# Layer 1's attention weights: transposed by VectorE in 32x32 squares and moved by transfers, mixed two blocks late

## The chip, the core and the metric

The kernel runs on one core of a Trainium2 chip. TensorE does matrix products into PSUM; VectorE (DVE), ScalarE (ACT) and GpSimd (POOL) do the rest; SyncE (SP), ACT and POOL also issue DMA transfers, each from its own in-order instruction queue. The metric is the device time of one execution in microseconds (us). Before the change its median was 2407.27 us over three runs (2404.34 to 2408.37).

## The reference

The input `x` is 8 batches of 256 channels on a 32x32 image, so 1024 tokens of 256 values in each batch, all in float32. Two layers follow each other.

Layer 0 is a linear attention block with 8 heads of 64, a softmax over the query index, an output projection and a residual. Layer 1 first normalizes each token and attends over the batch's own tokens, then adds a mixture of 8 experts with the best two for each token:

```python
def _L1_attn_ref(x, W):
    xa = jnp.einsum('bnd,ed->bne', x, W)
    scores = jnp.einsum('bne,bme->bnm', xa, x)
    attn = jax.nn.softmax(scores, axis=-1)
    y = jnp.einsum('bnm,bmd->bnd', attn, x)
    return y
...
t = _to_tokens(x)
t = t + _L1_attn_ref(_ln_t(t), L1_attn_W)
t = t + _L1_ffn_ref(_ln_t(t), L1_ffn_router_w, ...)
```

The change concerns `attn` in these lines: a 1024x1024 matrix in each batch. The product with `x` sums over the keys `m`, and TensorE sums over partitions, while the softmax sums over the free dimension. So the weights are made with the queries on partitions and are needed with the keys on partitions: they must be transposed.

## The kernel before, in words

A batch goes through layer 0 (`layer0`), layer 1's attention (`attend`), and the normalization and routing for the experts (`normed`, `dispatch`). Batches 0 to 6 send their tokens to the experts' rows in HBM; `experts` then runs once for all seven, and the last batch is done densely (`dense`) while the experts' results of the others are gathered, added and stored (`Results`).

`attend` splits the batch's 1024 queries into `NT = 8` blocks of 128. For a block `i`, `scores(i)` makes 128x1024 scores on TensorE in a PSUM tile of two banks (L670; the pool `ps_big` has three such tiles), VectorE takes the negated maximum of each row (`nmax`, L678), and ScalarE writes the exponentials to SBUF with their row sums (`ex`, L681, in the pool `expp`, which has six buffers of 128x1024 under the tag `exps`). `mix(i)` then has TensorE transpose the eight 128x128 squares of `ex` into a PSUM tile (`pa`, L689), VectorE copies them to SBUF (`aT`, L691), and TensorE makes eight products with the normalized tokens `n1` (`py`, L695). VectorE divides by the row sums and adds the residual (L699, L701). The loop at the end of `attend` runs `scores(i)` before `mix(i - 1)`, so a block is mixed one block late.

The token order inside a block is not the image's: a block of `NB = 4` has the tokens of one half of the batch (`NH2 = 2` halves of 512) that are congruent modulo 4. It makes 32x32 squares of the input and output images into transposes of VectorE: `SQ = 32`, `NQ = 4` groups of 32 partitions. `load_squares` and `residual` (L427, L434) and `store` (L1186, L1193) already use that.

`fill` calls put other work between: in batches 0 to 6 the next batch's value and query projections (`Begin.at`, lines `pv` L387 and `pqk` L328), in batch 7 the gathering and adding of the experts' results. The framework schedules the traced instructions into each engine's order and writes the semaphores. Every transfer issued from SP or ACT adds to one of eight semaphores, which are used in turn, and waits before it is issued until the transfer before it on the same semaphore has landed. In layer 0 of batches 1 to 7, SP also relays between TensorE's instructions (`relay`, L555).

Of the kernel before, what the change touches and what calls it, by code (L numbers as in the profile page):

```python
# [10 lines left out]
F32 = mybir.dt.float32  # L11
# [8 lines left out]
def kernel(  # L20
# [23 lines left out]
    nc = tc.nc  # L44
    P = 128
    B, C, S = x.shape
    E, D, FF = w1.shape
# [4 lines left out]
    NT = S // P  # L52
    NH2 = S // 512
# [14 lines left out]
    expp = ctx.enter_context(tc.tile_pool(name="expp", bufs=6))  # L68
# [6 lines left out]
    def big(name):  # L75

        return ps_big.tile([P, 1024], F32, tag="big", name=name)

    def acc(name):

        return ps_acc.tile([P, 512], F32, tag="acc", name=name)
# [54 lines left out]
    for e in range(E):  # L136
# [30 lines left out]
        fill=0.0,  # L167
# [41 lines left out]
    NB = NT // NH2  # L209
    SQ = 32  # L210
    NQ = P // SQ
# [40 lines left out]
    def layer_norm(t, dst, eps, name):  # L252
        return Norm(t, dst, eps, name).blocks(0, NT)

    def to_channels(t, dst, name):

        for cc in range(NCC):
            pt = big(f"pt_{name}_{cc}")
            for i in range(NT):
                nc.tensor.transpose(pt[:, ts(i, P)], t[:, i, ts(cc, P)], ident)  # L260
            copied = nc.vector.tensor_copy(dst[:, cc, :], pt)
        return copied
# [380 lines left out]
    def attend(b, t1, fill, tick=nothing):  # L643
        n1 = one.tile([P, NT, D], F32, tag="n", name=f"n1_{b}")
        layer_norm(t1, n1, 1e-5, f"a{b}")
        fill("norm 1")
        nT = one.tile([P, NCC, S], F32, tag="nT", name=f"nT_{b}")
        to_channels(n1, nT, f"n1_{b}")
        fill("normed 1")
        xa = one.tile([P, NCC, S], F32, tag="xa", name=f"xa_{b}")  # L650
        for ec in range(NCC):
            px = big(f"px_{b}_{ec}")
            for dc in range(NCC):
                for n in range(NH2):
                    nc.tensor.matmul(  # L655
                        px[:, ts(n, 512)],
                        WT[:, dc, ts(ec, P)],
                        nT[:, dc, ts(n, 512)],
                        start=(dc == 0),
                        stop=(dc == NCC - 1),  # L660
                    )
            tick(("xa", ec), nc.vector.tensor_copy(xa[:, ec, :], px))

        t2 = t1

        def scores(i):
            psc = big(f"ps1_{b}_{i}")
            for ec in range(NCC):
                for n in range(NH2):
                    nc.tensor.matmul(  # L670
                        psc[:, ts(n, 512)],
                        xa[:, ec, ts(i, P)],
                        nT[:, ec, ts(n, 512)],
                        start=(ec == 0),
                        stop=(ec == NCC - 1),
                    )
            nmax = small.tile([P, 1], F32, tag="nmax", name=f"nmax_{b}_{i}")
            tick(("max", i), nc.vector.tensor_reduce(nmax, psc, AX.X, ALU.max, negate=True))  # L678
            ex = expp.tile([P, 1024], F32, tag="exps", name=f"ex1_{b}_{i}")
            ssum = small.tile([P, 1], F32, tag="ssum", name=f"ssum_{b}_{i}")  # L680
            nc.scalar.activation(ex, psc, AF.Exp, bias=nmax, scale=1.0, accum_out=ssum)  # L681
            return ex, ssum

        def mix(i, ex, ssum):
            if i == NT - 1:
                fill("last weights")
            pt = big(f"pa_{b}_{i}")
            for m in range(NT):
                nc.tensor.transpose(pt[:, ts(m, P)], ex[:, ts(m, P)], ident)  # L689
            aT = two.tile([P, S], F32, tag="tr", name=f"aT_{b}_{i}")  # L690
            nc.vector.tensor_copy(aT, pt)  # L691
            ahead = fill("last products") if i == NT - 1 else None
            py = acc(f"py_{b}_{i}")
            for m in range(NT):
                nc.tensor.matmul(  # L695
                    py[:, :D], aT[:, ts(m, P)], n1[:, m, :], start=(m == 0), stop=(m == NT - 1)
                )
            rs = small.tile([P, 1], F32, tag="rs1", name=f"rs1_{b}_{i}")
            nc.vector.reciprocal(rs, ssum)  # L699
            with tc.issue_after(ahead.ins) if ahead else nullcontext():  # L700
                mixed = nc.vector.scalar_tensor_tensor(  # L701
                    t2[:, i, :], py[:, :D], rs, t1[:, i, :], ALU.mult, ALU.add
                )
            tick(("mixed", i), mixed)

        pending = None
        for i in range(NT):
            now = (i, *scores(i))
            if pending is not None:
                mix(*pending)  # L710
            pending = now
        mix(*pending)
        return t2


# [87 lines left out]
    def normed(b, t2, fill, tick=nothing, norm=None):  # L803

        if norm is None:
            n2 = one.tile([P, NT, D], F32, tag="n", name=f"n2_{b}")
            tick("normed", layer_norm(t2, n2, 1e-5, f"f{b}"))
        else:
            n2 = norm.dst
            tick("normed", norm.blocks(NT - 1, NT))  # L810
        fill("norm 2")
        nT = one.tile([P, NCC, S], F32, tag="nT", name=f"n2T_{b}")
        tick("turned", to_channels(n2, nT, f"n2_{b}"))

        nc.gpsimd.tensor_add(t2, t2, n2)  # L815
        fill("normed 2")
        l = logits(b, nT)
        return n2, nT, l
# [256 lines left out]
    class Results:  # L1075
# [94 lines left out]
        def tick(self, place, behind=None):  # L1170
            added, sent, stored = self.PLACES.get(place, (0, 0, 0))
            if added:
                with tc.issue_after(behind.ins):
                    for _ in range(added):
                        self.add()
            for _ in range(sent):
                self.gather(behind)
            for _ in range(stored):
                if self.whole:
                    b, total, n = self.whole.pop(0)  # L1180
                    store(b, total, n)
# [130 lines left out]
    for b in range(B):  # L1312
        xT = next_x
        if b + 1 < B:
            next_x = load_x(b + 1)
        if b > 0:
            xs = load_squares(b)
        t1 = layer0(b, xT, begun, routing, xs)
        if b + 1 < B:
            begun = Begin(b + 1, next_x)  # L1320
            t2 = attend(b, t1, begun.at)
            n2, _, l = normed(b, t2, begun.at)
            nc.sync.dma_start(groups[0].sums[b], t2)
            routing = dispatch(b, n2, l, groups[0])
            continue
        experts(groups[0])
        others = Results(groups[0])
        others.begin()
        norm = None

        def fill(place):

            nonlocal norm
            others.tick(place)
            if place == "last products":
                norm = Norm(t1, one.tile([P, NT, D], F32, tag="xa", name=f"n2_{b}"), 1e-5, f"f{b}")
                return norm.blocks(0, NT - 1)

        t2 = attend(b, t1, fill, others.tick)
        dense(b, t2, norm, others.tick)  # L1340
        assert others.added == len(others.units) and not others.whole
# [42 lines left out]
```

## Time and profile before

| what | value |
|---|---|
| median of three runs | 2407.27 us |
| the profiled execution | 2406.31 us |
| its span, first to last instruction | 2404.6 us |
| TensorE busy | 2359.7 us, 98% of the span |
| VectorE busy | 1540.9 us, 64% |
| ScalarE busy | 938.0 us, 39% |
| TensorE clock granted | 0.994 of full speed |
| transposes of the weights (`pa`) | 512 instructions, 273 ns each from start to end, overlapping |
| copies of them (`aT`) | 64 of 128x1024, median 1215 ns |
| one block of `attend`, batches 0 to 6 | 7.88 us |

Profile rows give the start in us from the span's beginning, the time, the engine, the line of the kernel, the operation, and the tiles written and read. PE is TensorE's products and PEld its weight loads; SPq and ACTq are instructions of a queue, such as the issue of a transfer. An arrow `<-` at the end says what released the engine from its wait. Each product of float32 appears as two MATMUL records. A time to landing goes from the issue until the data has arrived.

### The profile page before, as it was taken

The numbers are of one execution on the slowest core, as the hardware profiler recorded it, in microseconds if no ns is written. First come the engines' busy times: TensorE is split into PE (matmuls) and PEld (weight loads), VectorE is DVE, ScalarE is ACT, GpSimd is POOL, SyncE is SP. The second block draws the span as 40 slices with busy tenths as digits, with TensorE's granted clock in tenths as the row PEclk, the third lists the DMA queues.
The fourth block names the chain that finished last, engine by engine and source line by source line (L and its number), as shares of the span: only waits on it lengthen the run. The fifth ranks groups of instructions, "written<-read, shape, count | busy, mean of one in ns | idle before, by whom it ended". The sixth has DMA issues, their size and how long they took to land.

```text
span 2404.6 us, 36813 instructions
## 1 busy us (share of the span) xinstructions
PE 2359.7 (98%) x13759; PEld 1316.5 (55%) x13759; DVE 1540.9 (64%) x3660; ACT 938.0 (39%) x1570; POOL 420.0 (17%) x391
## 2 busy tenths in 40 slices
PE   9999999999999999999999999999999999999898
PEld 3356534654466336633664356435653388887565
DVE  5775587457845785578647864687468753334776
ACT  3651366126611662156315641465136622221111
POOL 0000012000200020003000200020002234444563
PEclk9999999999999999999999999999999999999899
DMA  8993201010101010001000100100010256665454
GB/s 294 386 386 101 53 19 36 1 36 12 43 1 35 8 47 1 18 18 54 1 18 18 47 8 6 31 25 12 1 36 19 74 176 220 219 219 161 142 170 119
DMA packets 114778, 196.59 MB, mean 82 GB/s; under 512 B 15752, under 2 KB 58408, under 8 KB 112808
## 3 DMA queue, kind: packets, MB, share of 16 engines
q1 hardware_dynamic: 88504, 126.52, 15.8%
q0 software_dynamic: 25008, 67.20, 9.1%
q8 instruction: 109, 1.79, 0.3%
q10 hardware_dynamic: 1088, 0.52, 0.1%
q14 instruction: 69, 0.57, 0.1%
HBM read 108.88 MB, written 110.90 MB: 91 GB/s over the span
## 4 chain that ended last, share of the span: by engine, by line
PE 91%; DVE 5%; ACT 2%; DMA 1%; issue 1%; POOL 0%; SPq 0%; DVEq 0%; ACTq 0%; POOLq 0%
PE po L545 19%; PE psc L468 18%; PE py L695 9%; PE ps L670 7%; PE pqk L350 7%; PE pr L636 5%; PE ph L1021 4%; PE pv L387 4%; PE pe L1046 4%; PE pdh L1250 2%; PE px L655 2%; PE pdy L1274 2%; PE pa L689 2%; PE pqk L328 2%; PE px L1011 1%
## 5 line engine op out<-in xcount | busy, mean ns | idle before, releaser
L509 ACT ACTIVATE ex<-psc,nmax 128x1024 f32<-128x1024 f32 x512 | 570.5, 1115 | 312.6 <-DVE scrap L492 227.8
L468 PE MATMUL psc<-qk,qk 64*64 64x512 f32 x4096 | 578.4, 594 | 10.3 <-ACT ex L509 10.3
L545 PE MATMUL po<-ex,vs 64*64 64x512 f32 x4096 | 573.5, 592 | 1.3 <-DVE vs L525 0.3
L492 DVE TENSOR_SCALAR_CACHE_REDUCE scrap<-psc,nmax 128x512 f32<-128x512 f32 x512 | 384.4, 751 | 152.0 <-PE psc L468 126.2
L483 DVE TENSOR_REDUCE nmax<-psc 128x1 f32<-128x512 f32 x512 | 350.3, 684 | 9.3 <-PE psc L468 9.3
L468 PEld LDWEIGHTS psc<-qk,qk 64*64 64x64 f32 x4096 | 181.0, 132 | 285.8 <-ACT ex L509 138.0
L545 PEld LDWEIGHTS po<-ex,vs 64*64 64x64 f32 x4096 | 177.9, 132 | 273.5 <-issue 81.7
L695 PE MATMUL py<-n,aT 128*128 128x256 f32 x1024 | 238.0, 386 | 2.9 <-DVE aT L691 2.9
L670 PE MATMUL ps<-nT,xa 128*128 128x512 f32 x512 | 236.0, 592 | 0.0
L695 PEld LDWEIGHTS py<-n,aT 128*128 128x128 f32 x1024 | 191.7, 191 | 66.6 <-DVE aT L691 41.8
L884 POOL DMA_INDIRECT rows<-n,d_at x112 | 108.8, 972 | 662.6 <-DVE nmax L483 662.3
L681 ACT ACTIVATE ex<-ps,nmax 128x1024 f32<-128x1024 f32 x64 | 71.3, 1115 | 348.0 <-DVE nmax L678 333.5
L815 POOL TENSOR_TENSOR t<-t,n 128x2048 f32<-128x2048 f32 x8 | 36.3, 4534 | 924.0 <-DVE n L242 924.0
L350 PE MATMUL pqk<-xT,wqkv 128*128 128x512 f32 x384 | 171.2, 599 | 0.0
L701 DVE SCALAR_TENSOR_TENSOR t<-py,rs,t 128x256 f32<-128x256 f32 x64 | 30.9, 482 | 194.4 <-PE py L695 194.4
L670 PEld LDWEIGHTS ps<-nT,xa 128*128 128x128 f32 x512 | 93.5, 190 | 81.2 <-issue 75.1
L350 PEld LDWEIGHTS pqk<-xT,wqkv 128*128 128x128 f32 x384 | 71.0, 190 | 99.9 <-issue 77.8
L1130 POOL DMA_INDIRECT yk<-y,yat x112 | 110.6, 988 | 72.4 <-issue 26.8
L636 PEld LDWEIGHTS pr<-wo,res 128*128 128x128 f32 x512 | 120.7, 331 | 3.7 <-ACT res L563 3.7
L636 PE MATMUL pr<-wo,res 128*128 128x256 f32 x512 | 121.6, 398 | 0.3 <-ACT res L563 0.3
L387 PE MATMUL pv<-wqkv,xT 128*128 128x512 f32 x256 | 120.3, 599 | 1.4 <-DVE v L395 1.0
L315 ACT ACTIVATE qk<-pqk,b_qks 128x512 f32<-128x512 f32 x124 | 85.6, 691 | 88.9 <-PE pqk L350 79.8
(189 smaller groups left out, 2479.8 us busy)
## 6 DMA issues: line engine op xcount, KB each, us to landing
rows<-wb SPq DMA_DIRECT2D x7, 8192.0 KB, 51.7
y<-yb SPq DMA_DIRECT2D x63, 256.0 KB, 2.4
xs<-in_x_dram SPq DMA_DIRECT2D x64, 128.0 KB, 3.9
out_dram<-oT SPq DMA_DIRECT2D x60, 128.0 KB, 2.9
xT<-in_x_dram SPq DMA_DIRECT2D x7, 1024.0 KB, 5.0
sums<-t SPq DMA_DIRECT2D x7, 1024.0 KB, 3.9
o<-sums SPq DMA_DIRECT2D x7, 1024.0 KB
wpack<-in_L_ffn_w_dram SPq DMA_DIRECT2D x4, 1024.0 KB
```

Source lines behind the costliest of these rows:

```text
L350: mm = nc.tensor.matmul(pq[:, ts(n, 512)], wqkv[:, cc, t, ts(g, P)], xT[:, cc, ts(n, 512)], start=(cc == 0), stop=(cc == NCC - 1),)
L387: nc.tensor.matmul(pv, self.xT[:, cc, ts(i, P)], wqkv[:, cc, 2, :], start=(cc == 0), stop=(cc == NCC - 1),)
L468: mm = nc.tensor.matmul(pss[at, h][ts(c, DK), ts(n, 512)], k[r, j * P + c * DK : j * P + (c + 1) * DK], q[r, ts(n, 512)], start=True, stop ...
L483: firsts[at, h] = nc.vector.tensor_reduce(nmax, pss[at, h][:, ts(0, 512)], AX.X, ALU.max, negate=True)
L492: seconds[h] = nc.vector.tensor_scalar(scrap, pss[at, h][:, ts(1, 512)], -1.0, nmaxes[at, h], ALU.mult, ALU.min, accum_out=nmax,)
L509: nc.scalar.activation(ex, pss.pop((at, h)), AF.Exp, bias=nmaxes.pop((at, h)), scale=1.0, accum_out=sums[at][:, h : h + 1],)
L545: mm = nc.tensor.matmul(po[n][ts(h, DK), :], vss[at][keys, h, :], exps[at, h][keys, ts(n, 512)], start=(j == 0 and turn == 0), stop=(j == ...
L636: nc.tensor.matmul(pr[:, :C], own(res[:, g, :], i), wo[:, g, :], start=(g == 0), stop=(g == NPAIR - 1))
L670: nc.tensor.matmul(psc[:, ts(n, 512)], xa[:, ec, ts(i, P)], nT[:, ec, ts(n, 512)], start=(ec == 0), stop=(ec == NCC - 1),)
L695: nc.tensor.matmul(py[:, :D], aT[:, ts(m, P)], n1[:, m, :], start=(m == 0), stop=(m == NT - 1))
L884: scatter = nc.gpsimd.indirect_dma_start(out=view[:, :], out_offset=bass.IndirectOffsetOnAxis(ap=ats[k][:, i : i + 1], axis=0), in_=n2[:, ...
L1130: ins = nc.gpsimd.indirect_dma_start(out=self.slot(at)[:, k, :], out_offset=None, in_=self.group.y[:, :], in_offset=bass.IndirectOffsetOnAxis(
```

## The change

The first seven blocks of a batch are transposed by `turn` rather than by TensorE. VectorE transposes each 32x32 square of `ex` in two instructions of 128x512, into a tile `sq`. Inside each square that is a full transpose, but the squares are still on the partitions of their old rows. Sixteen transfers of 32 partitions x 2 halves x 128 values move them to their places in a tile `aT`: those of row groups 0 and 2 are issued by SP, those of 1 and 3 by ACT. `mix` reads its eight 128x128 operands from `aT` with a stride. `ex`, `sq` and `aT` all come from the six buffers of the tag `exps`. A block is mixed two blocks late; the eighth block of a batch is transposed by TensorE as before (`turn_last`), after the loop.

```diff
-        def mix(i, ex, ssum):
-            if i == NT - 1:
-                fill("last weights")
+        def turn(i, ex):
+            sq = expp.tile([P, S], F32, tag="exps", name=f"sq_{b}_{i}")
+            to = sq.rearrange("p (n a q m) -> p n m a q", n=NH2, a=NQ, q=SQ)
+            since = ex.rearrange("p (n m a k) -> p n m a k", n=NH2, a=NQ, k=SQ)
+            for n in range(NH2):
+                nc.vector.transpose(to[:, n], since[:, n])
+            aT = expp.tile([P, S], F32, tag="exps", name=f"aT_{b}_{i}")
+            to, since = (t.rearrange("p (n c) -> p n c", n=NH2) for t in (aT, sq))
+            for a in range(NQ):
+                queue = (nc.sync, nc.scalar)[a % 2]
+                for k in range(NQ):
+                    queue.dma_start(to[ts(k, SQ), :, ts(a, P)], since[ts(a, SQ), :, ts(k, P)])
+            by = aT.rearrange("p (n q m) -> p n m q", n=NH2, q=P)
+            return [by[:, m // NB, m % NB] for m in range(NT)]
+
+        def turn_last(i, ex):
             pt = big(f"pa_{b}_{i}")
             for m in range(NT):
                 nc.tensor.transpose(pt[:, ts(m, P)], ex[:, ts(m, P)], ident)
             aT = two.tile([P, S], F32, tag="tr", name=f"aT_{b}_{i}")
             nc.vector.tensor_copy(aT, pt)
+            return [aT[:, ts(m, P)] for m in range(NT)]
+
+        def mix(i, aT, ssum):
             ahead = fill("last products") if i == NT - 1 else None
             py = acc(f"py_{b}_{i}")
             for m in range(NT):
                 nc.tensor.matmul(
-                    py[:, :D], aT[:, ts(m, P)], n1[:, m, :], start=(m == 0), stop=(m == NT - 1)
+                    py[:, :D], aT[m], n1[:, m, :], start=(m == 0), stop=(m == NT - 1)
                 )
...
-        pending = None
+        pending = []
         for i in range(NT):
-            now = (i, *scores(i))
-            if pending is not None:
-                mix(*pending)
-            pending = now
-        mix(*pending)
+            ex, ssum = scores(i)
+            if i < NT - 1:
+                pending.append((i, turn(i, ex), ssum))
+            if i > 1:
+                mix(*pending.pop(0))
+        fill("last weights")
+        pending.append((NT - 1, turn_last(NT - 1, ex), ssum))
+        for some in pending:
+            mix(*some)
```

## The prediction

> **What bounds the kernel now.** I read the page first: the engine totals and the chain that ended last.
>
> ```profile
> PE 2359.7 (98%) x13759; PEld 1316.5 (55%) x13759; DVE 1540.9 (64%) x3660; ACT 938.0 (39%) x1570; POOL 420.0 (17%) x391
> PE 91%; DVE 5%; ACT 2%; DMA 1%; issue 1%; POOL 0%; SPq 0%; DVEq 0%; ACTq 0%; POOLq 0%
> PE po L545 19%; PE psc L468 18%; PE py L695 9%; PE ps L670 7%; PE pqk L350 7%; PE pr L636 5%; PE ph L1021 4%; PE pv L387 4%; PE pe L1046 4%; PE pdh L1250 2%; PE px L655 2%; PE pdy L1274 2%; PE pa L689 2%; PE pqk L328 2%; PE px L1011 1%
> ```
>
> TensorE is the bound, and the work to be removed (`pa` L689) is 2% of its chain. So the first question is what the transposes cost TensorE, the second whether anything slower takes their place. Next I read the timeline of one block of layer 1's attention, in batch 0.
>
> ```profile
> 213.10 1.04 PE L689 MATMUL pa<-ident,ex 128*128 128x128 f32 x8
> 213.30 1.23 DVE L678 TENSOR_REDUCE nmax<-ps 128x1 f32<-128x1024 f32 x1 [0.56 <-PE ps L670]
> 213.97 1.88 PE L670 MATMUL ps<-nT,xa 128*128 128x512 f32 x4
> 214.44 1.22 DVE L691 COPY aT<-pa 128x1024 f32<-128x1024 f32 x1
> 215.71 3.72 PE L695 MATMUL py<-n,aT 128*128 128x256 f32 x16
> 219.27 1.88 PE L670 MATMUL ps<-nT,xa 128*128 128x512 f32 x4
> 220.98 1.04 PE L689 MATMUL pa<-ident,ex 128*128 128x128 f32 x8
> ```
>
> A block takes 7.88 us (213.10 to 220.98), all TensorE: eight transposes 0.87 (213.10 to 213.97), scores 3.4, products 3.4. VectorE is busy 3.6 of it and ScalarE 1.2, so both have room. Then ScalarE alone in the same batch: first two and last exponentials.
>
> ```profile
> 204.02 1.11 ACT L681 ACTIVATE ex<-ps,nmax 128x1024 f32<-128x1024 f32 x1
> 205.04 0.19 ACT L681 ACTIVATION_READ_ACCUMULATOR ex<-ps,nmax 128x1 f32 x1
> 206.18 1.12 ACT L681 ACTIVATE ex<-ps,nmax 128x1024 f32<-128x1024 f32 x1 [0.95 <-DVE rs L699]
> ...
> 254.04 1.11 ACT L681 ACTIVATE ex<-ps,nmax 128x1024 f32<-128x1024 f32 x1 [6.68 <-DVE nmax L678]
> ```
>
> Exponential 7 starts 50.0 us after exponential 0, in every batch; it waits for TensorE, never the reverse. Last, the rows nearest to the new operations: the store's transpose, four small transfers in a row on SP, two times to landing (of L1060, 256 KB, and of `out_dram`, 128 KB), and a wait of SP on an older transfer.
>
> ```profile
> L1186 DVE STREAM_TRANSPOSE oT<-o x14: 1941/2022/2120, 2218.0 to 2381.7; 128x1024 f32<-128x1024 f32 x14
> ```
>
> ```profile
> 2293.18 1.95 SPq L1193 DMA_DIRECT2D out_dram<-oT  x4
> ```
>
> ```profile
> DMA to landing us min/median/max: 2.2/2.4/3.5
> ```
>
> ```profile
> DMA to landing us min/median/max: 2.3/2.9/3.8
> ```
>
> ```profile
> SPq L427 <- DMA xT<-in_x_dram: 3.2, 2, 2.8
> ```
>
> An issue costs its queue some 0.49 us (1.95 / 4; the first, which had waited, 0.36), and a transfer waits for the one that last used its semaphore: eight semaphores go round.
>
> **The change part by part.** *Removed.* Of 8 blocks in each of 8 batches, 7 lose 8 transposes: 56 x 0.87 = 48.7 us of TensorE, 2.0% of the span, on its path. Their copies (1.215 each) go from VectorE, off the path.
>
> *Products.* `mix` now loads its weights from `aT` with a stride of 4 elements, where it read them in a row. The output projection does the same today, with the same shapes:
>
> ```profile
> 168.74 15.18 PE L636 MATMUL pr<-wo,res 128*128 128x256 f32 x64
> ```
>
> ```profile
> L636 PEld LDWEIGHTS pr<-wo,res x512: 307/332/332, 168.5 to 1937.8; 128*128 128x128 f32 x171
> ```
>
> ```profile
> L695 PEld LDWEIGHTS py<-n,aT x1024: 186/190/333, 207.7 to 2266.9; 128*128 128x128 f32 x171
> ```
>
> Its loads take 332 ns, those of `py` 190, and its products follow each other every 0.235 us (64 in 15.0 from first start to last), those of `py` every 0.216. So 16 records cost 0.3 more: 56 x 0.3 = 17 us go back to TensorE, net 0.57 a block saved.
>
> *Transposes on VectorE.* Two of 128x512 for a block. The store's row has the same strides (runs of 4 on the output side) and twice the size: half of 2.02 is 1.01, and 0.03 for an instruction of its own, so 2 x 1.04 = 2.08 us. The ends: 1.94 to 2.14 for a block (smallest store, largest transpose of `xs`). VectorE then has about 4.5 of a block's time: not the bound.
> The Trainium skill, "Vector Engine (DVE) Microarchitecture Reference", section 3.8, says that the 32x32 transpose sustains one element per cycle and lane. At the 0.96 GHz that "VectorE: DVE Perf Modes" gives, that would be an estimated 1.07 us for a block, not 2.08, and the sum below would come out about 55 us lower, and change its sign if all of that came out. The row of 2.02 for 1024 elements says half that rate; I go by the row.
>
> *Transfers.* 16 for a block, 8 on SP and 8 on ACT, 56 x 16 = 896 in all, each 32 KB in runs of 512 B. ACT's are in line with the exponentials. In the changed program's order ACT runs exponential i, then block i's eight transfers, then exponential i+1. The first of them waits for the block's transposes; behind it stands the next exponential, and for that wait block i+1's transposes, block i+3's scores (three PSUM buffers) and the mixing. Within the eight, ACT has four of the eight semaphores, so the fifth issue waits until the first has landed. No transfer from SBUF to SBUF is in the trace. Landing: from below, no end but the four issues themselves (1.85 us, where the wait vanishes); from above 3.9, the median of the loads of `xs` (128 KB). I take 2.2, the shortest of the 256 KB stores, since this is an eighth of that and only one short queue is ahead of it.
> A page speaks against the change here: "DMA: Bandwidth & Descriptors", section on the anatomy of one DMA, gives about 2.0 us fixed plus bytes / 436 GB/s, so an estimate of 2.08 for 32 KB, whose sum would be some 7 us lower than mine. No run here has yet shown such a transfer.
>
> *ACT's loop, then,* for one block: exponential with its accumulator read 1.21 (204.02 to 205.23), a handover 0.04, transposes 2.08, a handover 0.03, landing of the first four 2.2 + 0.05, the second four 1.95, a handover 0.05: **7.61 us**. (Handovers: the accumulator read ends at 215.82 and VectorE starts at 215.86; a store's transpose ends at 2395.90 and its issue starts at 2395.93; the third is an estimate from these.) TensorE needs 3.4 + 3.7 = 7.1, so it waits about 0.5 in each block, and the loop sets the end.
>
> *One batch.* Exponential 7 now comes 7 x 7.61 after exponential 0, plus about 0.7 since block 0's transposes stand behind `nmax` of block 1 (1.22, at 204.86): 54.0 for 50.0, so +4.0. What follows exponential 7 stays, but for 0.3 on the products of block 6, so +4.3: its own transposes on TensorE 0.87, the products of blocks 6 and 7, two fills of values. Block 6's last transfer was issued just before exponential 7 and lands beside the last transposes. So nothing is won back; TensorE's saving becomes waiting.
>
> ```profile
> 203.22 8.44 SPq L306 DMA_DIRECT2D wpack<-in_L_ffn_b_dram  x8
> ```
>
> ```profile
> 2229.00:2236.70 7.70, 7.70 (x34) 5.33 (x33) 7.16 (x12) 0.21 (x3) 5.85 (x6) 1.00 0.37 106
> ```
>
> These are SP's queue in batch 0, and the busy time of PE, PEld, DVE, ACT and POOL in one block of batch 7. Batches 1 to 6: 6 x 4.3 = 25.8. Batch 0: SP issues the weight packing until 211.66 (8.44 us from 203.22), while ACT could start block 0's transfers at about 208.2; block 0 is some 3.5 later: 7.8. Batch 7: VectorE is already busy 7.16 of 7.70 us there, with the others' results, and gains 2.08 - 1.215 for a block, while stores and gathers share queues and engines: 4.3 + 2 = 6.3.
>
> *Moved past on queues.* SP's loads of the next `x` and squares and its output stores in batch 7 now stand between these transfers; 0.49 each, loads needed only in the next batch's layer 0, hidden by 100 us and more of it. If that cover were gone, a batch would lose one landing, 4 us. POOL's queue is not passed. Mixing two late costs TensorE nothing by itself: scores of four blocks stand ahead of the first product.
>
> *Sum:* 25.8 + 7.8 + 6.3 = +39.9 on the profiled execution's 2406.31 (span 2404.6 and 1.7 around it; 1 us under the median of the three runs): 2446.2, so 2446.
>
> **The rivals.**
> *A, faster: the loop is shorter than 7.0 us.* At 7p + 1.0 = 50.0 a batch is even; below, TensorE's saving comes out, at most 7 x 0.57 = 4.0 a batch. It needs issues of 0.36 also when back to back, and a landing under 1.5: p = 1.21 + 0.04 + 2.08 + 0.03 + 2.88 + 0.05 = 6.29, where TensorE is the bound again; 6 x -4.0, -0.5 and -2 give -26.5: 2380 at best; with half of it, 2393. For it: 0.36 was seen after waits, and ACT's few issues were 0.38 to 0.46 long. Against: every run of issues in the trace falls to 0.49.
> *B, much slower: landings of 3.0* (the median 2.9 of `out_dram`, with sixteen transfers at once reading only 32 partitions each). p = 8.41, +9.9 a batch: 6 x 9.9 + 13.4 + 11.9 = +85: 2491. With 3.9, p = 9.31 and +16.2 a batch: about 2541. For it: medians of larger transfers. Against: those carry 4 to 8 times the bytes.
> *C, landing hidden, issue-bound:* p = 1.21 + 0.04 + 2.08 + 0.03 + 3.86 + 0.05 = 7.27, +1.9 a batch: 11.4 + 5.4 + 3.9 = +21: 2427.
>
> **How the numbers follow.** Forecast with a landing of 2.0 to 2.7 (2435 to 2474): 0.57. C: 0.19. B, above 2474: 0.12. A: 0.07. In between A and C, no difference: 0.05. What a measurement can tell here is 0.2%, 4.8 us. Range 2416 to 2488: it takes in C and the nearer half of B and leaves out A and B's far end. Faster 0.07, same 0.05, slower 0.88.
>
> **What would show it.** Right: exponentials about 7.6 us apart (was 7.88 on steady blocks, but 2.16 for the first), 51 to 56 from first to last; the fifth transfer on ACT starting when the first lands; TensorE idle before `py`, released by transfers; layer 0 unchanged; transposes of 1.0 to 1.1; loads of `py` near 330 ns. Wrong: transposes of 0.55 (the page), issues of 0.36, landings over 3, or a wait on SP in layer 0, where it relays for TensorE.

## The result, and the profile after

The changed kernel takes 2530.45 us (median of four runs, 2528.14 to 2532.07) against 2406.60 us before (four runs beside them): a ratio of 1.0511, 95% interval 1.0495 to 1.0526. It is 124 us slower. The forecast, 2446 with a range of 2416 to 2488, had the direction and missed the size.

The page of the changed kernel: its engine totals and its group of the products.

```profile
PE 2366.8 (94%) x13311; PEld 1332.8 (53%) x13311; DVE 1577.5 (62%) x3716; ACT 937.3 (37%) x1570; POOL 419.5 (17%) x391
...
L714 PE MATMUL py<-n,aT 128*128 128x256 f32 x1024 | 278.3, 431 | 64.6 <-DMA aT<-sq 53.2
```

TensorE has 448 transposes less, and is busy 7 us *more* than before (2359.7); its share falls from 98% to 94%. The records of the products take 278.3 us in all, where they took 238.0 before: with strided weights most are 0.40 us long instead of 0.38, and 156 of the 1024 (7 before) are over 0.55, the first behind a wait, or in stretches in which the profile shows half the clock (below). Of the products' 64.6 us of waits, 53.2 end with transfers. Where the 125.7 us of the span came from is read from the starts of the exponentials: exponential 0 to exponential 7 took 50.0 us in each batch before.

| | exponential 0 to 7 | from there to the next layer 0 | together, against before |
|---|---|---|---|
| batch 0 | 71.2 | 22.2 | +23.0 |
| batches 1 to 6 | 62.8 to 63.2 | 20.8 to 23.6 (20.4 before) | +13.1 to +16.0, in all +88.2 |
| batch 7 | 67.6 | 147.8 to the end of the span (151.0 before) | +14.5 |

Everything outside these stretches changed by 0.1 us in sum. The loop of eight blocks holds 116.0 of it, the stretch behind it 9.6. The loop itself stands in the timeline of ACT, batch 2 of the changed kernel (start, length, queue or engine, line, operation, idle time before it and what ended that):

```profile
756.58 1.11 ACT L681 ACTIVATE ex<-ps,nmax 128x1024 f32<-128x1024 f32 x1 [7.39 <-DMA aT<-sq]
757.59 0.19 ACT L681 ACTIVATION_READ_ACCUMULATOR ex<-ps,nmax 128x1 f32 x1
759.92 5.41 ACTq L697 DMA_DIRECT2D aT<-sq  x8
765.53 1.11 ACT L681 ACTIVATE ex<-ps,nmax 128x1024 f32<-128x1024 f32 x1 [7.75 <-DMA aT<-sq]
```

One block now takes 8.95 us (756.58 to 765.53). ACT runs the exponential, waits for VectorE's two transposes (757.81 to 759.85 in VectorE's timeline), issues eight transfers in 5.41 us, and can run the next exponential only then. In the waits of ACT's exponentials, 448.6 us in 56 waits end with these transfers.

The stretch behind exponential 7 is 20.8 us long in batches 1 and 4 and 22.2 to 23.6 in the others. Here is the granted clock of TensorE in it, batch 1 and then batch 2 (busy times of PE, PEld, DVE, ACT and POOL, then the clock, the DMA share and GB/s), and below the transposes of block 7 and the products of block 6 in the same two batches:

```profile
539.20:560.00 20.80, 19.53 (x94) 13.53 (x94) 10.87 (x23) 4.07 (x6) 4.54 (x1) 1.00 0.21 43
801.40:825.00 23.60, 22.34 (x92) 15.15 (x92) 10.87 (x23) 4.07 (x6) 4.53 (x1) 0.86 0.20 38
```

```profile
540.47 1.09 PE L705 MATMUL pa<-ident,ex 128*128 128x128 f32 x8 [3.16 <-ACT ex L681]
542.25 3.88 PE L714 MATMUL py<-n,aT 128*128 128x256 f32 x16
...
802.66 1.97 PE L705 MATMUL pa<-ident,ex 128*128 128x128 f32 x8 [4.92 <-ACT ex L681]
806.13 5.03 PE L714 MATMUL py<-n,aT 128*128 128x256 f32 x16
```

The clock records show 0.5 of full speed for 6.8 us behind exponential 7 in batches 2 and 5, for 3.4 us in batches 0, 3 and 6, and not at all in batches 1 and 4. These are the batches with +3.1 to +3.2, with +1.8 to +2.1 and with +0.4: the differences beyond 0.4, 10 us over the seven batches, go with the halved clock. In the kernel before, no such record falls into `attend` of batches 0 to 6.

The tile `aT` of the changed kernel shows what a transfer and a weight load cost:

```profile
L714 PEld LDWEIGHTS py<-n,aT x1024: 190/329/338, 228.6 to 2391.6; 128*128 128x128 f32 x171
...
L697 ACTq DMA_DIRECT2D aT<-sq x448: 592/609/867, 208.1 to 2381.9; - x150
L697 SPq DMA_DIRECT2D aT<-sq x448: 585/596/847, 222.0 to 2381.4; - x150
```

An issue is 0.60 to 0.61 us long at the median and 0.64 to 0.65 from start to start, on both queues. A transfer has landed 1.9 us after its issue starts at the median (1.77 at least, a quarter of ACT's after 2.1 or more; read from the updates of its semaphore). So four issues, 2.6 us, cover the landing of the first: in 54 of 56 blocks the fifth issue on ACT starts 0.65 to 0.67 us after the fourth, in two 0.97 and 1.02 after it.

Batch 0 adds a wait of its own. SP's queue in the changed kernel, timeline and then waits (line, what was waited for, us, times, longest):

```profile
210.11 0.65 SPq L295 DMA_DIRECT2D wpack<-in_L_ffn_w_dram  x1
210.80 2.25 SPq L300 DMA_DIRECT2D wpack<-b1T  x1
213.09 8.62 SPq L306 DMA_DIRECT2D wpack<-in_L_ffn_b_dram  x8
222.03 10.53 SPq L697 DMA_DIRECT2D aT<-sq  x16
```

```profile
SPq L295 <- DMA aT<-sq: 19.7, 1, 19.7
```

One weight packing transfer waited 19.7 us for one of ACT's new transfers, through the semaphore that both use in turn. SP was done with the packing at 221.7 instead of 211.66 and began with block 0's share only then; ACT's third exponential came 17.0 us after the second.

### The profile page after: what moved, and what is told of

It reads as the page before. It is cut to its first block, busy times and chain, and to the rows that moved or that the text cites. A ratio compares the mean times of both kernels' runs of the same rounds, so it can differ in the third digit from the quotient of the medians.

```text
span 2530.3 us, 37425 instructions
## 1 busy us (share of the span) xinstructions
PE 2366.8 (94%) x13311; PEld 1332.8 (53%) x13311; DVE 1577.5 (62%) x3716; ACT 937.3 (37%) x1570; POOL 419.5 (17%) x391
## 5 line engine op out<-in xcount | busy, mean ns | idle before, releaser
L492 DVE TENSOR_SCALAR_CACHE_REDUCE scrap<-psc,nmax 128x512 f32<-128x512 f32 x512 | 384.5, 751 | 152.2 <-PE psc L468 125.7
L714 PE MATMUL py<-n,aT 128*128 128x256 f32 x1024 | 278.3, 431 | 64.6 <-DMA aT<-sq 53.2
L714 PEld LDWEIGHTS py<-n,aT 128*128 128x128 f32 x1024 | 253.0, 311 | 118.6 <-issue 82.0
L681 ACT ACTIVATE ex<-ps,nmax 128x1024 f32<-128x1024 f32 x64 | 71.3, 1113 | 464.0 <-DMA aT<-sq 448.6
L691 DVE STREAM_TRANSPOSE sq<-ex 128x512 f32<-128x512 f32 x112 | 113.8, 1093 | 123.8 <-ACT ex L681 118.2
```

The source lines that it names most:

```text
L492: seconds[h] = nc.vector.tensor_scalar(scrap, pss[at, h][:, ts(1, 512)], -1.0, nmaxes[at, h], ALU.mult, ALU.min, accum_out=nmax,)
L691: nc.vector.transpose(to[:, n], since[:, n])
L714: nc.tensor.matmul(py[:, :D], aT[m], n1[:, m, :], start=(m == 0), stop=(m == NT - 1))
```

## The experiments

The theory after the comparison: **the blocks are set by ACT's loop, and in it by eight issues of 0.65 us.** The rivals: the landing of the transfers, which the products wait for; TensorE's products with a stride; the late mixing. A question beside it is why an issue costs 0.6 and not 0.49. The kernel before took 2406.1 to 2406.8 us beside all runs but one group, on a chip where it took 2423.8; there only ratios are compared.

**The price of an issue.** Groups of four transfers behind the kernel's last work, one form for each group:

```diff
+        for form in (cross, same, store_, load_, run1, full, whole, cross):
+            for q in (nc.scalar, nc.sync):
+                for j in range(4):
+                    form(q, j)
...
+                nc.vector.memset(dst, 0.0)
```

> The kernel before, with groups of four transfers put behind the last output product of the dense batch, each group alone on ACT and then on SP, a fill of the target tile between the groups: the change's own form (32 partitions x 2 runs of 512 B, SBUF to SBUF, to other partitions), the same to its own partitions, SBUF to HBM, HBM to SBUF, one run of 1 KB, 128 partitions x 2 runs, one run of 4 KB; at the end the change's form on both queues at once. Its time is not of interest; the start-to-start interval of the issues is. Theory 'the form costs it': the change's form takes 0.60 to 0.65 us per issue on either queue with the other one silent, and no more with both at work; transfers to or from HBM take 0.45 to 0.50. Rival 'the two queues hinder each other': 0.45 to 0.50 for all forms alone, over 0.6 only with both at work.

Measured, the instructions by line (duration in ns as min/median/max): the change's own form (L1316), HBM to SBUF in the same pieces (L1325), and one run of 4 KB (L1334), each with the other queue silent but for the last group of L1316.

```profile
L1316 ACTq DMA_DIRECT2D probe_dst<-probe_src x12: 592/610/1798, 2403.9 to 2490.8; - x12
L1316 SPq DMA_DIRECT2D probe_dst<-probe_src x8: 585/602/744, 2410.6 to 2485.1; - x8
...
L1325 ACTq DMA_DIRECT2D probe_dst<-probe_hbm x4: 566/586/605, 2433.8 to 2436.0; - x4
...
L1334 ACTq DMA_DIRECT2D probe_dst<-probe_src x4: 587/602/602, 2466.4 to 2468.3; - x4
```

The form costs it: 0.60 us at the median with one queue at work, and about as much with both (0.59 on SP, 0.60 to 0.61 and once 0.81 on ACT). That the two queues hinder each other is out. But the theory's second half failed: transfers from and to HBM cost 0.59 and 0.61 as well, in pieces of 32 partitions x 2 runs. A second group of forms was made to find the property that does it:

```diff
+            nc.scalar.dma_start(runs(dst)[ts(j, SQ)], rows(hbm)[j])
...
+            nc.scalar.dma_start(runs(dst)[ts(j, SQ), ::4, :], runs(hbm)[ts(j, SQ), ::4, :])
...
+            nc.scalar.dma_start(dst[:, ts(j, P)], src[:, ts(3 - j, P)])
```

> The kernel before with groups of four transfers on ACT behind its last work, each group of one form: HBM to SBUF with 32 partitions x 8 runs of 512 B (the form of the loads of x, 0.45 us in the trace before), 128 x 1, 32 x 1 and 32 x 2 runs; SBUF to SBUF with 128 x 1 run of 512 B, 128 x 1 run of 1 KB and 32 x 4 runs of 512 B; SBUF to HBM with 32 x 8 and 128 x 1 runs. Only the duration of an issue is of interest. If a small number of runs makes an issue long (64 runs 0.6, 256 runs 0.45): HBM to SBUF 32 x 8 at 0.45, 128 x 1 near 0.52, 32 x 1 over 0.6, and SBUF to SBUF by the same numbers. If SBUF on both sides makes it long: all SBUF to SBUF forms at 0.58 or more, whatever the number of runs, 128 x 1 and 32 x 4 among them.

```profile
L1320 ACTq DMA_DIRECT2D probe_dst<-probe_hbm x4: 309/462/472, 2407.0 to 2408.4; - x4
...
L1326 ACTq DMA_DIRECT2D probe_dst<-probe_hbm x4: 339/438/443, 2423.3 to 2424.6; - x4
...
L1329 ACTq DMA_DIRECT2D probe_dst<-probe_hbm x4: 597/616/687, 2430.6 to 2432.6; - x4
...
L1332 ACTq DMA_DIRECT2D probe_dst<-probe_src x4: 537/623/624, 2438.8 to 2440.7; - x4
```

These are, in order, HBM to SBUF with 32 x 8 runs, 32 x 1 and 32 x 2, and SBUF to SBUF with 128 x 1. The number of runs does not do it: 256 runs 0.46, 32 runs 0.44. From SBUF to SBUF every form of both groups took 0.54 to 0.71, even with one run for a partition (outside it: 0.47 for one, the first of its row; 0.74, 0.75 and 1.80 in the very first rows; the 0.81). To or from HBM it was 0.43 to 0.47 behind the first of a row where at least one side is in one piece for each partition (but 0.97 for one, in a row whose first took 1.54), and 0.56 to 0.69 where both sides are in pieces. Why, the runs don't show.

**Fewer issues on ACT, or none.** Four of a block's sixteen transfers on ACT and twelve on SP:

```diff
-                queue = (nc.sync, nc.scalar)[a % 2]
                 for k in range(NQ):
+                    queue = nc.scalar if a % 2 and k < 2 else nc.sync
```

> The changed kernel with 4 of the 16 transfers of a block on ACT and 12 on SP. Theory 'an issue costs its queue 0.65 us, and ACT's eight are in line with the exponentials': ACT's loop falls from 8.96 to 1.21 + 2.03 + 4 x 0.65 + 0.4 = 6.3 us, SP needs 12 x 0.65 = 7.8 for a block, and a block takes about 7.9: 7 blocks x 8 batches x 1.0 less, so about 2530 - 60 = 2470 (2450 to 2485). Rival 'the landing or TensorE's strided products hold the blocks': the same 16 transfers, the same products, so 2520 to 2540.

And all sixteen on SP (`queue = nc.sync`):

> The changed kernel with all 16 transfers of a block on SP. Theory 'an issue costs its queue 0.65 us': 16 x 0.65 = 10.4 us for a block against 8.96, 56 x 1.44 = +80: about 2610 (2590 to 2625). Rival 'only the blocking of ACT matters': ACT is free, a block falls to TensorE's 7.15, so under 2430. Rival 'landing or products': 2520 to 2540.

Measured: 2500.84 us (ratio 1.0389, 1.0371 to 1.0406) and 2628.97 us (1.0923, 1.0905 to 1.0941). Both outside the theory's range on the high side, by 16 and 4 us, and both the way it says, where each rival has another sign or none. SP's timeline in batch 2, first with twelve, then with sixteen:

```profile
735.21 56.71 SPq L697 DMA_DIRECT2D aT<-sq  x84
```

```profile
763.32 73.29 SPq L697 DMA_DIRECT2D aT<-sq  x112
```

SP issues without a pause, 0.675 and 0.654 us each, and it is now the bound. With twelve, ACT's loop is out of the way as computed (exponential 2 comes 5.98 us after exponential 1, exponential 3 6.24 after that; 49.8 from 0 to 7 instead of 62.8), but SP is behind by then, and the last products wait for it: 29 to 30 us from exponential 7 to the next layer 0 in batches 1 to 6, instead of 21 to 24. My estimate had counted the loop and forgotten that a queue with 56.7 us of work which starts 4 us after exponential 0 ends behind exponential 7.

**The same issues, out of the exponentials' way.** Block i's transfers stand behind exponential i + 1, so that ACT no longer waits for transposes in between:

```diff
                 queue = (nc.sync, nc.scalar)[a % 2]
-                for k in range(NQ):
-                    queue.dma_start(to[ts(k, SQ), :, ts(a, P)], since[ts(a, SQ), :, ts(k, P)])
+                with tc.issue_after(soft.ins):
+                    for k in range(NQ):
+                        queue.dma_start(to[ts(k, SQ), :, ts(a, P)], since[ts(a, SQ), :, ts(k, P)])
...
+            ex, ssum, soft = scores(i)
+            if i > 0:
+                at, sq, its = turned
+                pending.append((at, move(at, sq, soft), its))
...
```

> The changed kernel with the same 16 transfers on the same queues, but those of block i put behind exponential i+1 on ACT (and so on SP), so that the exponential no longer waits for transposes and issues in one chain. Theory 'ACT's loop': 1.21 + 8 x 0.65 + 0.3 = 6.7 us, below TensorE's 7.15, so TensorE is the bound again; the last block's transfers come later and cost 1 to 4 us at the end of a batch: 2390 to 2440. Rival 'landing': the products wait for transfers that start later still, so not below 2530. Rival 'strided products on TensorE': unchanged, 2520 to 2540.

Measured: 2444.25 us (1.0150, 1.0133 to 1.0167), 86 us less than the changed kernel with the same instructions in another order, and 4 above the range. ACT's timeline in batch 2:

```profile
754.78 1.11 ACT L681 ACTIVATE ex<-ps,nmax 128x1024 f32<-128x1024 f32 x1 [7.34 <-DVE nmax L678]
754.85 1.33 ACTq L701 DMA_DIRECT2D aT<-sq  x2
755.80 0.19 ACT L681 ACTIVATION_READ_ACCUMULATOR ex<-ps,nmax 128x1 f32 x1
756.22 4.07 ACTq L701 DMA_DIRECT2D aT<-sq  x6
762.02 1.11 ACT L681 ACTIVATE ex<-ps,nmax 128x1024 f32<-128x1024 f32 x1 [6.03 <-DVE nmax L678]
```

The exponential waits for `nmax` here, that is for TensorE, and the first transfers are issued while it runs. Over the run, 30 waits of the exponentials (173.4 us) end with `nmax` and 23 (148.6 us) still with transfers, where it was 1 and 56. In batches 1 to 6, exponential 7 comes 45.4 to 48.6 us after exponential 0, and `attend` costs +0.8 us a batch against before instead of +14.7. What is left sits in batch 0 (+16.5), in batch 7 (+9.2), and outside these stretches, mostly in layer 0 (+8.8 in all, not followed further). The landing as the cause is out: the transfers start later than in the changed kernel, and the time falls. So is TensorE with its strided loads, which are the same.

**Lateness alone.** The kernel before, all blocks on TensorE, mixed two blocks late:

```diff
+        exps, pending = [], []
         for i in range(NT):
+            exps.append(scores(i))
+            if i > 0:
+                pending.append((i - 1, turn(i - 1, exps[i - 1][0]), exps[i - 1][1]))
+            if i > 1:
+                mix(*pending.pop(0))
...
```

> The kernel before, all blocks transposed by TensorE as before, but mixed two blocks late, with the transposed weights in the buffers of the exponentials as in the changed kernel. Theory 'the issues in ACT's loop cost it all': lateness and buffers cost nothing by themselves, 2400 to 2412. Rival 'the late mixing holds buffers or the end of a batch': up to 2 us a batch or more, over 2420.

Measured: ratio 0.9974 (0.9962 to 0.9985), slightly *faster*. Exponential 7 comes 46.0 us after exponential 0 (455.01 and 500.97, batch 1), a block takes 7.76 instead of 7.88; behind it the product that was put off adds 3.3; together -0.73 us in each of batches 0 to 6. Batch 7 is 13.0 us longer than in the trace of the kernel before, but that is another chip: on the chip of this run, the kernel of the second run by way of HBM (below), whose batch 7 is as before, is 12.1 longer there too. Mixing late is no cost in batches 0 to 6, and at most about 1 us in batch 7.

**The stride alone.** The kernel before, with VectorE's copy writing the transposed weights in the changed kernel's order:

```diff
-            nc.vector.tensor_copy(aT, pt)
+            by = aT.rearrange("p (n q m) -> p n m q", n=NH2, q=P)
+            nc.vector.tensor_copy(by, pt.rearrange("p (n m q) -> p n m q", n=NH2, q=P))
...
```

> The kernel before, but VectorE's copy of the transposed weights writes them so that the products load their operands with a stride of 4 elements, as in the changed kernel. Nothing else. By the prediction's step, 64 blocks x 0.3 us = 19 us more: 2426 (2418 to 2436), loads of 330 ns. If the longer loads are covered by the products instead: 2404 to 2412. If the strided copy on VectorE is slow enough to bind: over 2440.

Measured: ratio 1.0295 (1.0278 to 1.0312). It is the third case, and the one that I had thought least of. One block in batch 0, from the timelines of TensorE and VectorE:

```profile
213.94 1.04 PE L689 MATMUL pa<-ident,ex 128*128 128x128 f32 x8
214.81 1.88 PE L670 MATMUL ps<-nT,xa 128*128 128x512 f32 x4
217.45 4.11 PE L696 MATMUL py<-n,aT 128*128 128x256 f32 x16 [0.76 <-DVE rs L700]
221.40 1.88 PE L670 MATMUL ps<-nT,xa 128*128 128x512 f32 x4
```

```profile
215.28 2.12 DVE L692 COPY aT<-pa 128x1024 f32<-128x1024 f32 x1
```

From the first product to the next scores it is 3.95 us where it was 3.56 (215.71 to 219.27 in the prediction's block): **0.39 a block for the strided loads**, predicted 0.3. The rest is VectorE: its copy takes 2.12 instead of 1.22 with the strided output, it stands between the transposes and the products, and the products start 0.90 later.

**The order of the columns.** That pointed at the change's own transposes, which write with a stride of 4 elements. The changed kernel with runs of 32 elements in `sq` and `aT`:

```diff
-            to = sq.rearrange("p (n a q m) -> p n m a q", n=NH2, a=NQ, q=SQ)
+            to = sq.rearrange("p (n m a q) -> p n m a q", n=NH2, a=NQ, q=SQ)
...
-            to, since = (t.rearrange("p (n c) -> p n c", n=NH2) for t in (aT, sq))
+            to, since = (t.rearrange("p (m c) -> p m c", m=NT) for t in (aT, sq))
...
-                    queue.dma_start(to[ts(k, SQ), :, ts(a, P)], since[ts(a, SQ), :, ts(k, P)])
+                    queue.dma_start(to[ts(k, SQ), :, ts(a, SQ)], since[ts(a, SQ), :, ts(k, SQ)])
```

> The changed kernel with another order of the columns: each square is kept as 32 runs of 32 elements, so a transfer moves 32 partitions x 8 runs of 128 B, and the products read their operands in a row (loads of 190 instead of 330 ns, 0.3 us less of TensorE for a block). Same 16 transfers, same queues, same order. Theory 'ACT's loop': TensorE is not the bound in the blocks, so the time stays, 1.045 to 1.057 of the kernel before, as long as the issue of the form stays at 0.6 us. Rival 'strided products on TensorE': 17 us come out, 1.044 or less.

Measured: 2513.31 us (1.0443, 1.0428 to 1.0458), 17 less than the changed kernel. By the time alone it is between the theory's 1.045 and the rival's 1.044, and the interval takes in both; the trace decides. The tile `sq`, and ACT's timeline in batch 2:

```profile
L697 ACTq DMA_DIRECT2D aT<-sq x448: 592/624/1393, 207.2 to 2364.2; - x150
...
L691 DVE STREAM_TRANSPOSE sq<-ex x112: 662/674/712, 205.8 to 2358.1; 128x512 f32<-128x512 f32 x112
```

```profile
758.79 1.11 ACT L681 ACTIVATE ex<-ps,nmax 128x1024 f32<-128x1024 f32 x1 [7.51 <-DMA aT<-sq]
759.81 0.19 ACT L681 ACTIVATION_READ_ACCUMULATOR ex<-ps,nmax 128x1 f32 x1
761.41 5.51 ACTq L697 DMA_DIRECT2D aT<-sq  x8
767.13 1.11 ACT L681 ACTIVATE ex<-ps,nmax 128x1024 f32<-128x1024 f32 x1 [7.13 <-DMA aT<-sq]
```

A transpose of 128x512 takes 0.67 us instead of 1.09, so ACT's wait for two of them falls from 2.14 to 1.41 (759.81 + 0.19 to 761.41), the issues rise by 0.1, and the block falls from 8.96 to 8.34. The exponential still waits for the transfers, not for TensorE: it is ACT's loop that became shorter.

**By way of HBM.** SP stores a block's tile to HBM and loads it back in four transfers, five issues for a block, none on ACT; in all batches, and in batches 1 to 6 alone:

```diff
-            for a in range(NQ):
-                queue = (nc.sync, nc.scalar)[a % 2]
-                for k in range(NQ):
-                    queue.dma_start(to[ts(k, SQ), :, ts(a, P)], since[ts(a, SQ), :, ts(k, P)])
+            via = turned[i % 4]
+            nc.sync.dma_start(via, sq)
+            since = via.rearrange("(a s) (k c) -> a k s c", s=SQ, k=NQ)
+            for a in range(NQ):
+                nc.sync.dma_start(aT[:, ts(a, 256)], since[a])
...
```

> The changed kernel with another way for the squares: SP stores the whole tile of a block to HBM in one transfer of 128 partitions and loads it back in four of 128 partitions x 1 KB, five issues for a block and none on ACT; the products then read with a stride of 8. Theory 'issues and ACT's loop': ACT's loop is 1.2, SP needs about 0.5 + 2.9 + 4 x 0.45 + 0.2 = 5.4 us, TensorE 7.15, so TensorE is the bound again in batches 1 to 6; batches 0 and 7 lose some: 2385 to 2415. Rival 'landing holds the blocks': two landings in a row for each block instead of one, over 2530.

> As the run by way of HBM, but batches 0 and 7 transpose on TensorE and mix one block late as in the kernel before. Theory 'issues': 6 x 7 x 0.57 = 24 us less than before if nothing comes late at a batch's end: 2383 (2375 to 2398), below both kernels. Rival 'landing': 2480 to 2530.

Measured: ratios of 1.0889 (1.0871 to 1.0908) and 1.0644 (1.0626 to 1.0662). On the other chip's 2406.6 that is 2621 and 2562, over 200 and 160 us above what was expected: here the transfers do hold the blocks. ACT's waits in the second of them:

```profile
ACT ex L683 <- DMA turned<-sq: 157.8, 17, 10.0
```

While only loads run (751 to 756 us), 93 GB/s are moved, so a block's 512 KB take 5.6 us (last three columns: granted clock, mean busy share of the 16 DMA engines, GB/s):

```profile
751.00:756.00 5.00, 5.00 (x17) 3.49 (x16) 2.21 (x4) 0.00 (x0) 0.00 (x0) 0.93 0.26 93
```

The share of 0.26 is as much as four of the 16 engines at work. The landings say the same: each of these loads shows one update of its semaphore 0.9 us after its issue starts and then four more, the stores show 16. Of the first four stores issued behind such loads in batch 2, three landed 5.7 to 7.3 us after their issue (in the third, twelve updates came within 2.9 us and the last four after 7.0), and an exponential waits for that store to free its buffer.

A third form, each load with 32 partitions x 4 runs instead of 128 partitions x 1 (the line that differs; the loads that follow are written to match):

```diff
-            since = via.rearrange("(a s) (k c) -> a k s c", s=SQ, k=NQ)
+            since = via.rearrange("(a s) (k c) -> k s a c", s=SQ, k=NQ)
```

> As the run by way of HBM in batches 1 to 6, but each of the four loads writes 32 partitions x 4 runs of 1 KB instead of 128 partitions x 1 run. In the run before this, the loads ran at some 90 GB/s and took 5 to 6 us together, as if on few engines. Theory 'the loads were on few engines': they land in 2.5 us, SP needs 0.4 + 2.6 + 4 x 0.65 = 5.6 for a block, TensorE is the bound: 0.988 to 1.000 of the kernel before. Rival 'the way through HBM is too long whatever the form': over 1.04.

Measured: 2441.33 us (1.0137, 1.0123 to 1.0152), above the theory's range and below the rival's, 0.05 less of the ratio than the form before it: its loads show 16 updates each and land in 3.0 us at the median, exponential 7 comes 6 us earlier than in the kernel before. But the end of a batch takes 10 to 11 us more. In SP's queue two loads of the next `x` stand ahead of the loads of each of the last three blocks; whether that is the cause was not tried, and the way by HBM was not followed further.

**A version from these parts.** Batches 1 to 6 only, blocks 0 to 5 only, transfers behind the next exponential; blocks 6 and 7, and batches 0 and 7, on TensorE as before. First with the stride of 4, then with runs of 32 elements. The new lines of the first, against the version with the transfers behind the next exponential (its lines that go are left out):

```diff
+        squares = NT - 2 if 0 < b < B - 1 else 0
         for i in range(NT):
             ex, ssum, soft = scores(i)
             if i > 0:
                 at, was, its = turned
+                now = move(at, was, soft) if at < squares else turn_last(at, was)
+                pending.append((at, now, its))
+            turned = (i, turn(i, ex) if i < squares else ex, ssum)
+            if len(pending) > (squares > 0):
+                mix(*pending.pop(0))
```

> Batches 1 to 6: the transfers of a block behind the next exponential, as in the run of the changed kernel with that order, but only for blocks 0 to 5; blocks 6 and 7 are transposed by TensorE. Batches 0 and 7 as in the kernel before. Theory 'issues': the first blocks keep the gain of that run (exponential 7 comes 2 to 4 us earlier than before) and the end of a batch loses 1 to 2 us rather than 4: 0.992 to 0.999 of the kernel before. Rival 'transfers hinder the products anyway': over 1.002.

> As the run with batches 1 to 6 and blocks 0 to 5, with the squares kept as runs of 32 elements, so that the products read in a row. If the loads' 0.3 us a block are on TensorE's path there: 6 x 6 x 0.3 = 11 us less than with the stride of 4, 0.987 to 0.994 of the kernel before. If transfers with runs of 128 B take longer to issue or to land: no gain over it, or a loss.

Measured: 2403.12 us (0.9985, 0.9977 to 0.9994) and **2371.89 us (0.9857, 0.9843 to 0.9871)**, 34.7 us below the kernel before and 158.6 below the changed one. The second is better than its range. Its page, chain and products:

```profile
PE 2321.6 (98%) x13471; PEld 1287.2 (54%) x13471; DVE 1537.9 (65%) x3696; ACT 937.4 (40%) x1570; POOL 419.4 (18%) x391
...
PE 87%; DVE 5%; DMA 3%; SPq 2%; issue 1%; ACT 1%; ACTq 1%; DVEq 0%; POOLq 0%
...
L717 PE MATMUL py<-n,aT 128*128 128x256 f32 x1024 | 234.5, 383 | 3.2 <-DVE aT L710 2.9
```

TensorE is the bound again and its products wait 3.2 us in the whole span (21.2 with the stride, 17.9 of them for transfers). A batch gains 5.3 to 6.6 us, 6.0 at the mean. That is what the parts say: six transposes saved, 6 x 0.87 = 5.2, and 0.73 from lateness. With the stride, 6 x 0.39 = 2.3 a batch go to longer loads, and most of the rest to waits.

## Why the prediction was wrong in size

*The path was right in the main.* The forecast said that ACT runs exponential i, block i's eight transfers, then exponential i + 1; that this loop takes TensorE's place; and that nothing of the saved transposes comes back. Its formula, 7p + 0.7 - 50.0 with p for one block on ACT, gives +13.4 with the measured 8.96; measured were +12.7 to +13.2 in batches 1 to 6. That the loop is the cause was shown by taking it away with the same instructions (86 us less).

*The step that failed* is "An issue costs its queue some 0.49 us", and with it the term "landing of the first four 2.2 + 0.05, the second four 1.95". The eight issues took 5.41 us, not 4.20. The 0.49 came from a row of stores to HBM, read as the price of any issue; the same trace had no transfer from SBUF to SBUF, and for landing I gave bounds from both sides, but for the issue only a better case, 0.36, and none worse. Of p's excess of 1.35 this is 1.21. The rest is handovers: the semaphore instructions between the three took 0.31 (0.03, 0.08, 0.20) where I had 0.12. In batches 1 to 6, with seven intervals each, the excess is 6 x 7 x 1.35 = 57 us by this sum of the 62 that were missing there (88.2 for 25.8). As measured, the loops hold 53 of the 62 and the ends of the batches 9. The eight issues on SP gave no relief, being as slow.

*Landing* was 1.9 us at the median, so my 2.2 was too long, and the wait for it that the forecast put into the loop was not there: the fifth issue did not start when the first transfer landed, as the signs of being right had it, but behind the fourth issue. The Trainium skill, "DMA: Bandwidth & Descriptors", section on the anatomy of one DMA, has a formula that makes it an estimated 2.08 for 32 KB, which is nearer than mine and also too long; it stands there for transfers of GpSimd's path, and these were issued by SP and ACT. Rival B, landings of 3.0 and more, gave 2491 to 2541: the size of what came, by a mechanism that was not there. Rival C had the mechanism, "landing hidden, issue-bound", with the wrong price: at 0.65 an issue its loop is 1.21 + 2.03 + 5.41 + 0.31 = 8.96. Rival A needed cheaper issues and fell with them.

*The transposes* were right: 2.03 for a block against 2.08, from the store's row, which has the same stride. The Trainium skill, "Vector Engine (DVE) Microarchitecture Reference", section 3.8, whose rate makes an estimated 1.07 for a block, is not met with the stride of 4. With runs of 32 elements a block takes 1.35, and that may be the same rate: from the two sizes with the stride of 4 (1.09 us for 512 elements, 2.02 for 1024) I estimate a fixed 0.16 us an instruction, and 1.35 less two of these is 1.03. What I didn't see is that the stride itself cost the row a third of its time.

*The strided loads* were under-sized, 0.39 measured for 0.3 predicted, but hidden in the changed kernel, since TensorE waits there in any case.

*Batch 0* was +23.0 for 7.8. I took SP to be free at 211.66; it was held until 221.7 because a packing transfer waited for ACT's transfer on the shared semaphore. I had noted that semaphores go round, and applied it only to ACT's own. The trace shows this wait; no run took it away by itself. *Batch 7* was +14.5 for 6.3: the same excess in the loop, 7 x 1.35 = 9.4, is more than the difference (its loop was 17.6 longer than before, what follows 3.2 shorter).

*The end of a batch* was +0.4 in batches 1 and 4, where I had 0.3, and +1.8 to +3.2 in the other five, in which the granted clock is halved for 3.4 or 6.8 us there. The forecast had no term for the clock; it is 10 us of the 124. TensorE's wait just before the transposes was 2.5 to 5.0 us in these five batches and 3.2 in the two others, so its length alone does not tell them apart; what brings the lower clock on, no run tested. *Lateness costs nothing*: right, it even gains 0.73 a batch.

## What to carry to other kernels

An instruction queue that issues transfers is an engine like the others: count its issues by a row of the same form and the same two memories, and where no such row exists, take a bound above the known price as well as one below. Then look at what stands behind the issues in that queue: here the kernel with the same 896 transfers was 124 us slower than before with ACT's ahead of the next exponential, and 38 with them behind it. And when a layout is chosen for a transfer, price its stride on every engine that writes or reads it, since an element order that cost the transfers 0.1 us for eight issues gave VectorE and TensorE back 0.7 and 0.4 us for a block.

## What the runs showed of the hardware

- An issue on SP's or ACT's queue took 0.43 to 0.47 us between HBM and SBUF with one side in one piece for each partition, behind the first of a row (0.31 to 0.39), and mostly 0.58 to 0.63 from SBUF to SBUF or with both sides in pieces, whether one queue or both were at work. One form lies between: the loads from HBM to 128 partitions, 1 KB for each, took 0.51 to 0.66.
- VectorE writing float32 with a stride of 4 elements: the 32x32 transposes of 128x512 took 1.09 us, and 0.67 to 0.69 in runs of 32; a copy of 128x1024 from PSUM 2.06, and 1.22 in a row.
- Weight loads of 128x128 float32 with a stride of 4 or 8 elements took 0.33 us, 0.19 in a row; eight pairs of products then took 0.39 us longer (stride of 4).
- Loads from HBM to 128 partitions, one run of 1 KB for each, ran at 93 GB/s, with a busy share of the 16 DMA engines of 0.26 and four landing updates each besides the early one; the same data as 32 partitions x 4 runs had 16 updates each and landed in 3.0 us at the median. How a transfer is cut into partitions and runs decided here on how many engines it ran, and how fast.
- TensorE's granted clock was 0.5 for 3.4 to 10.2 us at a time in `attend` of the changed kernel, and never there in batches 0 to 6 of the kernel before. Eight transposes then took 1.97 us instead of 1.09.
